# The last attention block's ending moved out of a branch and beside the following convolution; two weight sets and one table given other times and places

## The chip, the cores and the metric

The kernel runs on one core of one Trainium2 chip. The metric is the time of one execution in device microseconds (us). The engines are named as in the profile: PE (TensorE, with PEld for its weight loads), DVE (VectorE), ACT (ScalarE), POOL (GpSimd) and SP (SyncE, which here only issues DMA transfers). L-numbers are lines of the kernel before.

## What is computed

Four layers run one after another on two images of 128 channels and 64 x 64 pixels (L = 4096 positions). Only the end of layer 0, the start of layer 1 and one weight set of layer 2 matter here. Cut to that, the reference is:

```
# layer 0: group norm, rotary attention with 4 heads of 32 channels, projection, residual
xi = group_norm(x).reshape(b, c, L)
q, k, v = split(einsum('oc,bcl->bol', w_qkv, xi) + b_qkv)
q, k = rotary(q), rotary(k)                      # t * cos + swap(t) * sin
weight = softmax(einsum('bct,bcs->bts', qh * scale, kh * scale))
a = einsum('bts,bcs->bct', weight, vh).reshape(b, c, L)
x = xi + einsum('oc,bcl->bol', w_proj, a) + b_proj

# layer 1 (its start): a 3x3 convolution 128 -> 64 with GELU (the stem), then a wide 9x9 one, and others
h = gelu(affine(conv2d(x, cv1_w, 1)))
o0 = silu(affine(conv2d(h, conv0_w, 4)))
...

# layer 2: three residual steps with two 3x3 convolutions, weights w1 and w2
for _ in range(3):
    x = x + (conv(relu(conv(x, w1) + b1), w2) + b2) / 3
```

## The kernel before, in words

The image stays in memory all the time as `xa` (128 channels on the partitions, both images, with a border of one pixel).

**Prologue of layer 0** (`layer0`, 0 to 102 us). SP loads the two images in quarters (`load_x`, L121) and the table of cosines and sines in eight slices (`load_cs`, L124) into the tile `cs`, 32 KB per partition. ACT's queue loads the small weights, among them `wvT`, `wprojT` (L88) and `wproj3` (L90; only the branch that is not taken uses it). DVE takes the statistics (L143), ACT normalises, and for 16 steps PE multiplies q and k, DVE rotates them with the cosines (L186, L188), POOL adds (L190, into five buffers rt3) and SP stores them to DRAM. The values of the first image are split into three bf16 parts and a column of ones (`v3[0]`, `v3[1]`; POOL sets the ones, L136, two memsets).

**The branch.** A flag computed from the data decides between `attend` (taken) and `attend_any` (L297). Everything inside is one unit: nothing outside the branch is put between its instructions, and behind it every engine jumps over the code of the other side.

**`attend`** goes over image b, head h, block qb of 512 queries and 32 blocks kb of 128 keys, in groups of three kb, in an order written out by hand. For a group PE makes the scores (L382), ACT the exponentials (L388), and two groups later PE accumulates the weighted values (L398). Since `v3` has columns of ones, the accumulator has three partial sums of 32 rows and the denominators in the last 32. At kb = 31 `normalise` makes the quotient of the head: a reciprocal (L409), two copies, three products on DVE (L415), two additions on POOL (L416, L417) into `att`. When all four heads of a block are there, `project` multiplies with `wpt` (PE, L424) and DVE adds the residual and the bias `bo` to `xa` (L426); this is done at kb = 24 of the next block, and for the very last block (b = 1, qb = 7) behind the loop, with nothing beside it. SP fetches pieces of q and k for the next head into a ring of two (`stg`), POOL and DVE split them (L346, L353). The second image's values are made inside this loop (`late_values`, for h = 1 and 2 of the first image).

**Behind the branch** (`body`, then `layer1`). ACT's queue loads `w1T` (L1964), and DVE makes layer 2's first weights `u1` of it (`quad_weights`, ten instructions, L1093 to L1102). SP loads the stem's weights `cv1T` (L588) into memory that later is `comb[5]`, then the wide convolution's weights `conv0T` in 18 loads (L595) and stores the image for later (`xs`, L597). POOL clears the border of `hz` (L600). Then, in an order written out by hand, the stem goes over eight blocks of eight rows: 36 matmuls each (L627), a Gelu on ACT (L632); between the blocks DVE prepares the wide convolution's weights (`wide_weights`, L607 to L618) and combinations of the stem's output (`combine`, L644 to L651). The wide convolution's products follow on PE (L667). The stem's block k reads rows 8k - 1 to 8k + 8 of both images.

Of the kernel before, what the change touches and what calls it, by code (L numbers as in the profile page):

```python
# [10 lines left out]
F32 = mybir.dt.float32  # L11
F16 = mybir.dt.float16
# [8 lines left out]
P = 128  # L21
# [53 lines left out]
def layer0(g, I):  # L75
# [6 lines left out]
    with ExitStack() as ctx:  # L82
# [3 lines left out]
        nc.scalar.dma_start(wv, I["wvT"])  # L86
        wpt = w.tile([P, P], F32, name="wpt")
        nc.scalar.dma_start(wpt, I["wprojT"])  # L88
        wp3 = w.tile([96, NH, P], F32, name="wp3")
        nc.scalar.dma_start(wp3, I["wproj3"])  # L90
        flag = w.tile([1, 1], I32, name="flag")
        bo = w.tile([P, 1], F32, name="bo")

# [8 lines left out]
        with ExitStack() as pctx:  # L102
# [11 lines left out]
            top = pw.tile([P, NB, 2, NBLK], F32, name="top")  # L114
            cs = pw.tile([P, NBLK, 2, BLK], F32, name="cs")

# [14 lines left out]
            for k in range(1, NBLK):  # L131
                load_cs(k)
            bv = pw.tile([P, 1], F32, name="bv")
            nc.scalar.dma_start(bv, I["bv"].unsqueeze(1))
            for b in range(NB):
                nc.gpsimd.memset(v3[b][:, :, :, 3 * CH :], 1.0)  # L136

# [159 lines left out]
        with tc.If(small > 0) as cond:  # L297
            attend(g, v3, wv, wpt, bo, qd, kd, q4, qk, stg)
        with cond.Else():
            with tc.tile_pool(name="l0vs", bufs=2) as vs, tc.tile_pool(name="l0vp", bufs=2, space=PSUM) as vp:  # L300
                for k in range(NBLK):
                    late_values(g, v3, vp.tile([P, BLK], F32, name="pv"), vs, wv, 1, k)
            attend_any(g, v3, wp3, bo, qd, kd, q4)

# [5 lines left out]
def fetch(g, stg, src, n, c):  # L310

    b, h = divmod(n, NH)
    t = stg.tile([P, PIECE], F32, name="piece")
    for r in range(4):
        g.nc.sync.dma_start(
            t[r * CH : (r + 1) * CH], src[b][h * CH : (h + 1) * CH, c * PIECE : (c + 1) * PIECE]
        )
    return t


# [40 lines left out]

def attend(g, v3, wv, wpt, bo, qd, kd, q4, qk, stg):

# [5 lines left out]
    with ExitStack() as ctx:  # L369
# [23 lines left out]
        def weigh(group, e):  # L393
            nonlocal acc
            for i, (b, h, qb, kb) in enumerate(group):
                if kb == 0:
                    acc = psa.tile([P, BLK], F32, name="acc")
                nc.tensor.matmul(acc, v3[b][:, kb, h, :], e[:, i, :], start=(kb == 0), stop=(kb == NS - 1))  # L398
                if kb == NS - 1:
                    normalise(b, h, qb, acc)  # L400
                    if h == NH - 1:
                        done.append((b, qb))

        def normalise(b, h, qb, acc):

            if qb == h == 0:
                att[b] = ap.tile([P, L], F32, name="att")
            rec = sm.tile([96, BLK], F32, name="rec")
            nc.vector.reciprocal(rec[0:32], acc[96:128])  # L409
            nc.vector.tensor_copy(rec[32:64], rec[0:32])  # L410
            nc.vector.tensor_copy(rec[64:96], rec[0:32])
            parts = sm.tile([CH, 3, BLK], F32, name="parts")
            for j in range(3):
                rows = slice(32 * j, 32 * j + 32)
                nc.vector.tensor_tensor(parts[:, j, :], acc[rows], rec[rows], ALU.mult)  # L415
            nc.gpsimd.tensor_add(parts[:, 0, :], parts[:, 0, :], parts[:, 1, :])  # L416
            nc.gpsimd.tensor_add(  # L417
                att[b][h * CH : (h + 1) * CH, qb * BLK : (qb + 1) * BLK], parts[:, 0, :], parts[:, 2, :]
            )

        def project(b, qb):

            pp = psa.tile([P, BLK], F32, name="acc")
            nc.tensor.matmul(pp, wpt, att[b][:, qb * BLK : (qb + 1) * BLK], start=True, stop=True)  # L424
            xv = interior(g, b, qb * RB, RB)
            nc.vector.scalar_tensor_tensor(xv, img(pp), bo, xv, ALU.add, ALU.add)  # L426

# [12 lines left out]
        ]  # L440
        held, done, coming = [], [], []
        with tc.manual_schedule():
            for c in range(1, 4):
                split_less(g, qk[0], 1, c, q4[1][:, c * PIECE : (c + 1) * PIECE], nc.vector)
            for u in range(0, len(units), GR):
                group = units[u : u + GR]
                b, h, qb, kb = group[0]
                held.append((group, scores(group)))
                if done and 24 <= kb < 24 + GR:
                    project(*done.pop(0))  # L450
                if len(held) > LAG:
                    weigh(*held.pop(0))
                if b == 0 and 1 <= h <= 2 and qb in (0, 5, 6, 7) and 24 <= kb < 24 + GR:
                    k = 4 * (h - 1) + (0, 5, 6, 7).index(qb)
                    late_values(g, v3, psa.tile([P, BLK], F32, name="acc"), sm, wv, 1, k)
                if 4 <= kb < 4 + GR:
                    coming = [(n, j, c, fetch(g, stg, (qd, kd)[j], n, c)) for n, j, c in pieces(b * NH + h, qb)]
                elif 26 <= kb < 26 + GR:
                    for n, j, c, t in coming:
                        split(g, qk[n % 2], j, c, t)  # L460
                    coming = []
            for x in held:
                weigh(*x)
            for x in done:
                project(*x)


def attend_any(g, v3, wp3, bo, qd, kd, q4):

    nc, tc = g.nc, g.tc  # L470
    NS = L // P
    with ExitStack() as ctx:
        big = ctx.enter_context(tc.tile_pool(name="l0big", bufs=1))
        sm = ctx.enter_context(tc.tile_pool(name="l0sm", bufs=2))
        at = ctx.enter_context(tc.tile_pool(name="l0at", bufs=2))
        pss = ctx.enter_context(tc.tile_pool(name="l0ps2", bufs=2, space=PSUM))
        pst = ctx.enter_context(tc.tile_pool(name="l0pst", bufs=2, space=PSUM))
        pso = ctx.enter_context(tc.tile_pool(name="l0pso", bufs=1, space=PSUM))
        id16 = big.tile([P, P], F16, name="id16")
        nc.vector.tensor_copy(id16, g.ident)  # L480

        for b in range(NB):
# [34 lines left out]
            for qt in range(NS):  # L517
                aT = sm.tile([96, NH, P], F32, name="aT")
                for h in range(NH):
                    s16, nm, e16 = scores(qt, h)  # L520
                    nc.scalar.activation(e16, s16, AF.Exp, bias=nm)
                    pt = at.tile([P, NS, P], F16, name="pt")
                    for j in range(4):
# [15 lines left out]
                xv = interior(g, b, qt * 2, 2)  # L539
                nc.vector.scalar_tensor_tensor(xv, img(pp), bo, xv, ALU.add, ALU.add)  # L540

# [23 lines left out]
def stem_and_wide(g, I, hz, fw, early, ahead):  # L565
# [14 lines left out]
    with ExitStack() as ctx:  # L580
# [6 lines left out]
        cw = comb[5].rearrange("p q r i -> p (q r i)")[:, : 9 * 64].rearrange("p (t o) -> p t o", o=64)  # L587
# [1350 lines left out]
def body(ctx, tc, I, out, layers=(0, 1, 2, 3), dump=None):  # L1938
# [156 lines left out]
```

## Time and profile before

| what | value |
|---|---|
| median of 3 runs | 5540.79 us (5538.51 to 5542.69) |
| the profiled execution | 5536.55 us |
| its span in the profile | 5534.8 us |
| mean granted PE clock | 0.886 |
| busy PE, DVE, ACT, POOL | 85%, 82%, 74%, 66% of the span |
| attention, first score to last accumulation | 103.1 to 1038.1 us |
| stem (L627) | 1056.4 to 1121.3 us |
| wide convolution, first product | 1121.3 us |

The span is the time from the first to the last instruction on the core; the rest of the execution's time lies around it. "Busy" sums an engine's instructions over the span, so it is an average over stages with different limits. The chain of waits follows the work that ended last backwards; a row of it gives start, length and what it was. In a group's row, `out<-in` are the tiles, `x` the number of instructions, then follow busy time, the mean of one in ns, and the idle time before them with what ended it. Queue rows (PEldq, SPq and so on) are the instructions of an engine's sequencer, such as jumps, semaphore waits and DMA issues.

### The profile page before, as it was taken

The page shows a single profiled execution, that of the slowest core. Times are in us where ns is not written, and L with a number is a line of the kernel's source. Part 1 is how long each engine was busy: PE and PEld are TensorE (multiplying, and loading weights), DVE is VectorE, ACT ScalarE, POOL GpSimd, SP SyncE. Part 2 cuts the span into 40 slices and gives each one's busy share as a digit, 9 for nine tenths or more (in the row PEclk, how much of TensorE's full clock was granted, in tenths as well). Part 3 has the DMA queues.
Part 4 walks back from the last instruction along what each step waited for, and adds up shares of the span by engine and source line. Part 5 has one row for each costly group of instructions (what it writes and reads, how often), then busy time and mean ns, then how long its engine had stood idle before and what let it go on. Part 6 is the DMA issues. An engine that isn't in the chain of part 4 may idle for free.

```text
span 5534.8 us, 54557 instructions
## 1 busy us (share of the span) xinstructions
PE 4701.0 (85%) x17062; PEld 1747.6 (32%) x17062; DVE 4548.0 (82%) x4253; ACT 4072.5 (74%) x6257; POOL 3646.3 (66%) x1196
## 2 busy tenths in 40 slices
PE   7999999899987899778888778778888777788776
PEld 3444444344443343222222222222222222222221
DVE  7665555551346996899999999999999999999998
ACT  4999999500346213798888888888888888888886
POOL 5222222100001211899999999999999999999998
PEclk9999999999998999888787888887887889888887
DMA  4111111300563000655655555555565565555554
GB/s 169 43 46 31 31 31 39 62 1 16 110 108 75 10 0 6 147 128 127 148 130 132 138 141 127 134 143 131 139 144 132 127 146 132 133 135 142 138 131 103
DMA packets 335737, 554.27 MB, mean 100 GB/s; under 512 B 69600, under 2 KB 116208, under 8 KB 335440
## 3 DMA queue, kind: packets, MB, share of 16 engines
q1 hardware_dynamic: 334032, 549.27, 41.8%
q8 instruction: 135, 2.21, 0.2%
q10 hardware_dynamic: 1408, 1.46, 0.1%
q14 instruction: 162, 1.33, 0.1%
HBM read 461.40 MB, written 89.13 MB: 99 GB/s over the span
## 4 chain that ended last, share of the span: by engine, by line
DVE 45%; PE 35%; ACT 10%; issue 5%; DMA 2%; POOL 1%; SPq 0%; DVEq 0%; POOLq 0%; ACTq 0%
DVE db L1682 30%; DVE db L1646 11%; PE ps L382 8%; PE acc L398 8%; PE m L1236 6%; PE m L667 4%; ACT da L1668 4%; PE acd L973 2%; DVE gt L1709 1%; ACT db L1674 1%; PE m L627 1%; PE pf L936 1%; ACT L1533 1%; ACT u L1533 1%; PE m L806 1%
## 5 line engine op out<-in xcount | busy, mean ns | idle before, releaser
L1692 POOL TENSOR_TENSOR db<-db,c 128x2048 f32<-128x2048 f32 x512 | 2312.5, 4531 | 45.6 <-ACT hl L1687 32.2
L1668 ACT ACTIVATE da<-dd,am 128x512 f32<-128x512 f32 x2048 | 1398.1, 687 | 301.1 <-DVE db L1682 280.4
L1682 DVE TENSOR_TENSOR_SCAN db<-da,db 128x512 f32<-128x512 f32 x1376 | 1583.9, 1201 | 34.5 <-ACT db L1674 26.9
L388 ACT ACTIVATE e<-ps 128x1536 f16<-128x1536 f32 (+1 forms) x683 | 919.7, 1601 | 23.2 <-PE ps L382 23.2
L1682 DVE TENSOR_TENSOR_SCAN db<-da,hl,db 128x512 f32<-128x512 f32 x672 | 825.9, 1271 | 40.9 <-POOL db L1655 2.8
L1646 DVE TENSOR_TENSOR db<-pbc,dd 128x2048 f32<-128x2048 f32 (+1 forms) x384 | 779.6, 2030 | 31.8 <-DMA dd<-dx 31.8
L1655 POOL TENSOR_TENSOR db<-b,dd 128x2048 f32<-128x2048 f32 (+1 forms) x192 | 772.9, 4026 | 14.0 <-DMA b<-bx 14.0
L1700 PE MATMUL py<-db,fold 128*32 128x512 f32 x4096 | 610.7, 682 | 150.9 <-POOL db L1692 150.8
L382 PE MATMUL ps<-q 128*128 128x512 f16 x2048 | 553.0, 378 | 3.4 <-issue 2.1
L398 PE MATMUL acc<-e,v 128*128 128x512 f16 x2048 | 552.9, 379 | 0.1
L416 POOL TENSOR_TENSOR parts<-parts 32x512 f32<-32x512 f32 x64 | 80.4, 1257 | 666.3 <-DVE parts L415 650.3
L1674 ACT ACTIVATE db<-da,db,hl 128x1 f32<-128x1 f32 x1120 | 393.7, 352 | 147.4 <-DVE db L1646 103.5
L1287 POOL MEMSET v<- 128x256 f32 x2 | 1.1, 550 | 699.7 <-DVE b L1125 699.7
L1236 PE MATMUL m<-v,u 128*128 128x512 f32 x864 | 378.1, 600 | 42.9 <-DVE v L1179 41.3
L409 DVE RECIPROCAL rec<-acc 32x512 f32<-32x512 f32 x64 | 214.9, 3358 | 212.0 <-PE acc L398 211.7
L1593 PE MATMUL pm<-dd,ident 128*128 128x512 f32 x512 | 356.5, 834 | 2.9 <-ACT dd L1586 2.7
L1625 PE MATMUL pbc<-bc,sel 64*128 64x512 f32 x384 | 208.7, 543 | 127.7 <-DVE db L1646 126.9
L1552 PE MATMUL pm<-u,wxp 128*72 128x512 f32 x256 | 191.3, 890 | 141.0 <-ACT u L1533 141.0
L382 PEld LDWEIGHTS <-q 128*128 128x128 f16 x2048 | 197.3, 97 | 273.4 <-issue 92.8
L398 PEld LDWEIGHTS <-v 128*128 128x128 bf16 x2048 | 199.0, 97 | 248.4 <-issue 9.1
L1700 PEld LDWEIGHTS py<-db,fold 128*32 128x32 f32 x4096 | 90.4, 114 | 542.9 <-issue 309.3
L1528 PE MATMUL pm<-xn,wcs 128*128 128x512 f32 x512 | 235.1, 602 | 18.5 <-ACT xa L1727 7.3
(342 smaller groups left out, 6575.7 us busy)
## 6 DMA issues: line engine op xcount, KB each, us to landing
dd<-dx SPq DMA_DIRECT2D x1024, 256.0 KB, 6.5
dx<-dd SPq DMA_DIRECT2D x128, 512.0 KB, 5.5
c<-bx SPq DMA_DIRECT2D x1024, 64.0 KB, 2.1
b<-bx SPq DMA_DIRECT2D x512, 64.0 KB, 4.6
early<-pos SPq DMA_DIRECT2D x104, 256.0 KB, 9.8
piece<-qd SPq DMA_DIRECT2D x128, 128.0 KB, 2.7
piece<-kd SPq DMA_DIRECT2D x112, 128.0 KB, 2.7
hats<-pos SPq DMA_DIRECT2D x32, 256.0 KB, 9.8
```

Source lines behind the costliest of these rows:

```text
L382: nc.tensor.matmul(ps[:, i, :], t[:, 1, kb * P : (kb + 1) * P], t[:, 0, qb * BLK : (qb + 1) * BLK], start=True, stop=True,)
L388: nc.scalar.activation(e[:, :n, :], ps[:, :n, :], AF.Exp, scale=1.0 / UP**2)
L398: nc.tensor.matmul(acc, v3[b][:, kb, h, :], e[:, i, :], start=(kb == 0), stop=(kb == NS - 1))
L1236: nc.tensor.matmul(m[x], weights[j][:, dy, x, :], v[j][b][:, x, r0 : r0 + RP, :].rearrange("p r i -> p (r i)"), start=(dy == 0), stop=(dy ...
L1593: nc.tensor.matmul(ps, g.ident, S[i]["dd", hf][:, x, :], start=(x == 0), stop=(x == 1))
L1646: nc.vector.tensor_tensor(db_tile(k)[:, :, :n], G[k].pop("pb")[:, :n].unsqueeze(1).to_broadcast([P, 4, n]), S[i]["d4", hf][:, 1, :, :n], A ...
L1655: nc.gpsimd.tensor_tensor(db_tile(k)[:, :, n:], S[i]["b", ng][:, n:].unsqueeze(1).to_broadcast([P, 4, BLK - n]), S[i]["d4", hf][:, 1, :, n ...
L1668: nc.scalar.activation(da, S[i]["d4", hf][:, 0, q, :], AF.Exp, scale=am[:, hf, q, ng : ng + 1])
L1674: nc.scalar.activation(b0, da[:, first : first + 1], AF.Identity, bias=b0, scale=hl[:, hf, ng, q, :])
L1682: nc.vector.tensor_tensor_scan(d1, d0, d1, 0.0 if zero else hl[:, hf, ng, q, :], ALU.mult, ALU.add)
L1692: nc.gpsimd.tensor_mul(v, v, S[i]["c", ng].unsqueeze(1).to_broadcast([P, 4, BLK]))
L1700: nc.tensor.matmul(S[i]["y", hf][32 * q : 32 * q + 32, :], fold, G[k]["db"][:, q, :], start=False, stop=(ng == NNG - 1),)
```

## The change

- **The last block's ending.** `normalise` and `project` become functions of the module. In the branch, the last block's first three heads are normalised into `g.heads` instead of `att`; of the last head ACT only copies the accumulator, denominators included, to `g.last`. Behind the branch, ahead of the stem's first block, DVE and POOL normalise it into `g.heads` with the stem's later buffers as scratch. After the stem's second block (k = 1) PE projects, DVE adds the residual, and SP stores the second image (`xs[1]`), which before was stored together with the first.
- **The stem's weights.** `cv1T` is loaded at the start of the kernel, on SP's queue behind the cosines, into `g.cw`.
- **One tile for all of it.** `g.lead`, 1728 columns, lives from before layer 0 to the end of layer 2: columns 0 to 575 are `cw`, 576 to 1087 `last`, 1088 to 1599 `heads`, the rest `wpt`. All of it later serves as `comb[5]`. `u1` and `bo` live there too now.
- **Layer 2's weights.** `w1T` is fetched in three parts (three taps of 128 columns each) into the ring of the q and k pieces, in the blocks qb = 5, 6, 7 of the first image's last head, and each part is made into weights there.
- **The cosines.** `cs` is no tile of its own but the memory of `v3[1]`, seen as float32. The ones of `v3[1]` are set by POOL at the start of `attend`.
- **Smaller ones.** `wproj3` is loaded only in the branch that is not taken. The scratch of `late_values` shares a ring with the reciprocals. The other branch sets `last` and `heads` so that the ending adds only the bias.

The core of the diff:

```
 def layer0(g, I):
-        wpt = w.tile([P, P], F32, name="wpt")
+        wpt, bo = g.wpt, g.bo
         nc.scalar.dma_start(wpt, I["wprojT"])
-        wp3 = w.tile([96, NH, P], F32, name="wp3")
-        nc.scalar.dma_start(wp3, I["wproj3"])
-        bo = w.tile([P, 1], F32, name="bo")
...
-            cs = pw.tile([P, NBLK, 2, BLK], F32, name="cs")
+            cs = v3[1].bitcast(F32).rearrange("p s h d -> p (s h d)").rearrange("p (k i c) -> p k i c", k=NBLK, i=2)
...
                 load_cs(k)
+            nc.sync.dma_start(g.cw, I["cv1T"])
...
-            for b in range(NB):
-                nc.gpsimd.memset(v3[b][:, :, :, 3 * CH :], 1.0)
+            nc.gpsimd.memset(v3[0][:, :, :, 3 * CH :], 1.0)

+def residual_taps(g, I, pool, y):
+    t = pool.tile([P, PIECE], F32, name="piece")[:, : 3 * P].rearrange("p (x o) -> p x o", o=P)
+    g.nc.sync.dma_start(t, I["w1T"][:, 3 * y : 3 * y + 3, :])
+    return t
+def residual_weights(g, y, t):
+    quad_weights(g, g.u1[:, y : y + 1], t.unsqueeze(1), 1.0)
+def normalise(g, acc, rec, parts, dst):
+    nc = g.nc
+    nc.vector.reciprocal(rec[0:32], acc[96:128])
+    nc.vector.tensor_copy(rec[32:64], rec[0:32])
+    nc.vector.tensor_copy(rec[64:96], rec[0:32])
+    for j in range(3):
+        rows = slice(32 * j, 32 * j + 32)
+        nc.vector.tensor_tensor(parts[j], acc[rows], rec[rows], ALU.mult)
+    nc.gpsimd.tensor_add(parts[0], parts[0], parts[1])
+    nc.gpsimd.tensor_add(dst, parts[0], parts[2])
+def project(g, b, qb, pp, att):
+    g.nc.tensor.matmul(pp, g.wpt, att, start=True, stop=True)
+    xv = interior(g, b, qb * RB, RB)
+    g.nc.vector.scalar_tensor_tensor(xv, img(pp), g.bo, xv, ALU.add, ALU.add)

 def late_values(g, v3, pv, pool, wv, b, k):
-    v32 = pool.tile([P, 4, NH, CH], F32, name="v32")
+    v32 = pool.tile([P, BLK], F32, name="rec").rearrange("p (c h d) -> p c h d", c=4, h=NH)

 def attend(g, I, v3, wv, qd, kd, q4, qk, stg):
+        def finish(b, h, qb, acc):
+            final = (b, qb) == (NB - 1, NBLK - 1)
+            if final and h == NH - 1:
+                nc.scalar.copy(g.last, acc)
+                return
+            to = g.heads if final else att[b][:, qb * BLK : (qb + 1) * BLK]
+            rec = sm.tile([P, BLK], F32, name="rec")
             parts = sm.tile([CH, 3, BLK], F32, name="parts")
+            normalise(g, acc, rec, [parts[:, j, :] for j in range(3)], to[h * CH : (h + 1) * CH])
+            if h == NH - 1:
+                done.append((b, qb))
...
         with tc.manual_schedule():
+            nc.gpsimd.memset(v3[1][:, :, :, 3 * CH :], 1.0)
...
                 if 4 <= kb < 4 + GR:
                     coming = [...]
+                    if (b, h) == (0, NH - 1) and qb >= 5:
+                        taps = qb - 5, residual_taps(g, I, stg, qb - 5)
                 elif 26 <= kb < 26 + GR:
...
+                    if taps:
+                        residual_weights(g, *taps)
+                        taps = None
             for x in held:
                 weigh(*x)
-            for x in done:
-                project(*x)

 def stem_and_wide(g, I, hz, fw, early, ahead):
-        comb = [early[:, i] for i in range(5)] + [a.tile([P, NQ, CR, NF], F32, name="comb5")]
-        cw = comb[5]...
-        nc.sync.dma_start(cw, I["cv1T"])
+        comb = [early[:, i] for i in range(5)] + [g.lead.rearrange("p (q r i) -> p q r i", q=NQ, r=CR)]
+        cw = g.cw
...
-        for b in range(NB):
-            nc.sync.dma_start(g.xs[b].rearrange("c (h w) -> c h w", w=HW), interior(g, b))
+        nc.sync.dma_start(g.xs[0].rearrange("c (h w) -> c h w", w=HW), interior(g, 0))
...
         with tc.manual_schedule():
+            s, p, d, q = spdq[0]
+            normalise(g, g.last, s, [t[0:CH] for t in (p, d, q)], g.heads[3 * CH :])
             for k in range(NBLK):
                 stem(k)
+                if k == 1:
+                    project(g, NB - 1, NBLK - 1, ps.tile([P, BLK], F32, name="m"), g.heads)
+                    nc.sync.dma_start(g.xs[1].rearrange("c (h w) -> c h w", w=HW), interior(g, 1))

 def body(ctx, tc, I, out, layers=(0, 1, 2, 3), dump=None):
-    if 0 in layers:
+    with tc.tile_pool(name="l2w", bufs=1) as pool:
+        g.u1 = pool.tile([P, 3, 6, P], F32, name="u1")
+        g.bo = pool.tile([P, 1], F32, name="bo")
+        g.lead = pool.tile([P, 1728], F32, name="lead")
+        g.cw = g.lead[:, : 9 * 64].rearrange("p (t o) -> p t o", o=64)
+        g.last = g.lead[:, 576:1088]
+        g.heads = g.lead[:, 1088:1600]
+        g.wpt = g.lead[:, 1600:]
         layer0(g, I)
-    with tc.tile_pool(name="l2w", bufs=1) as pool:
-        with tc.tile_pool(name="l2stage", bufs=1) as stage:
-            raw = stage.tile([P, 9, P], F32, name="raw")
-            nc.scalar.dma_start(raw, I["w1T"])
-            g.u1 = pool.tile([P, 3, 6, P], F32, name="u1")
-            quad_weights(g, g.u1, raw.rearrange("p (y x) o -> p y x o", x=3), 1.0)
```

More of the change, by code (lines that the diff above doesn't have):

```diff
@@ L297, in layer0 @@
         with tc.If(small > 0) as cond:
-            attend(g, v3, wv, wpt, bo, qd, kd, q4, qk, stg)
+            attend(g, I, v3, wv, qd, kd, q4, qk, stg)
         with cond.Else():
+            nc.gpsimd.memset(v3[1][:, :, :, 3 * CH :], 1.0)
             with tc.tile_pool(name="l0vs", bufs=2) as vs, tc.tile_pool(name="l0vp", bufs=2, space=PSUM) as vp:
@@ L302, in layer0 @@
                     late_values(g, v3, vp.tile([P, BLK], F32, name="pv"), vs, wv, 1, k)
-            attend_any(g, v3, wp3, bo, qd, kd, q4)
+                for y in range(3):
+                    residual_weights(g, y, residual_taps(g, I, vs, y))
+            nc.vector.memset(g.last[0:96], 0.0)
+            nc.vector.memset(g.last[96:128], 1.0)
+            nc.vector.memset(g.heads, 0.0)
+            attend_any(g, I, v3, qd, kd, q4)
 PIECE = L // 4
@@ L359, in split, with attend @@
     split_less(g, qk, j, c, t, g.nc.vector)
-def attend(g, v3, wv, wpt, bo, qd, kd, q4, qk, stg):
+def attend(g, I, v3, wv, qd, kd, q4, qk, stg):
     nc, tc = g.nc, g.tc
@@ L399, in weigh @@
                 if kb == NS - 1:
[L400 to L404, printed above, removed]
+                    finish(b, h, qb, acc)
+        def finish(b, h, qb, acc):
             if qb == h == 0:
                 att[b] = ap.tile([P, L], F32, name="att")
[L408 to L411, printed above, removed]
-            parts = sm.tile([CH, 3, BLK], F32, name="parts")
[L413 to L426, printed above, removed]
+            final = (b, qb) == (NB - 1, NBLK - 1)
[4 more added lines that the diff above has]
+            rec = sm.tile([P, BLK], F32, name="rec")
+            parts = sm.tile([CH, 3, BLK], F32, name="parts")
+            normalise(g, acc, rec, [parts[:, j, :] for j in range(3)], to[h * CH : (h + 1) * CH])
+            if h == NH - 1:
+                done.append((b, qb))
         def pieces(n, qb):
@@ L441, in attend @@
         held, done, coming = [], [], []
+        taps = None
         with tc.manual_schedule():
+            nc.gpsimd.memset(v3[1][:, :, :, 3 * CH :], 1.0)
             for c in range(1, 4):
@@ L449, in attend @@
                 if done and 24 <= kb < 24 + GR:
-                    project(*done.pop(0))
+                    b0, q0 = done.pop(0)
+                    project(g, b0, q0, psa.tile([P, BLK], F32, name="acc"), att[b0][:, q0 * BLK : (q0 + 1) * BLK])
                 if len(held) > LAG:
@@ L461, in attend, with attend_any @@
                     coming = []
+                    if taps:
+                        residual_weights(g, *taps)
+                        taps = None
             for x in held:
                 weigh(*x)
-            for x in done:
-                project(*x)
-def attend_any(g, v3, wp3, bo, qd, kd, q4):
+            assert not done
+def attend_any(g, I, v3, qd, kd, q4):
     nc, tc = g.nc, g.tc
@@ L475, in attend_any @@
         at = ctx.enter_context(tc.tile_pool(name="l0at", bufs=2))
+        tp = ctx.enter_context(tc.tile_pool(name="l0tp", bufs=1))
         pss = ctx.enter_context(tc.tile_pool(name="l0ps2", bufs=2, space=PSUM))
@@ L478, in attend_any @@
         pso = ctx.enter_context(tc.tile_pool(name="l0pso", bufs=1, space=PSUM))
+        wp3 = big.tile([96, NH, P], F32, name="wp3")
+        nc.scalar.dma_start(wp3, I["wproj3"])
         id16 = big.tile([P, P], F16, name="id16")
@@ L521, in attend_any @@
                     nc.scalar.activation(e16, s16, AF.Exp, bias=nm)
-                    pt = at.tile([P, NS, P], F16, name="pt")
+                    pt = tp.tile([P, NS, P], F16, name="pt")
                     for j in range(4):
@@ L539, in attend_any @@
                 xv = interior(g, b, qt * 2, 2)
-                nc.vector.scalar_tensor_tensor(xv, img(pp), bo, xv, ALU.add, ALU.add)
+                if b == NB - 1 and qt >= NS - BLK // P:
+                    nc.vector.tensor_add(xv, xv, img(pp))
+                else:
+                    nc.vector.scalar_tensor_tensor(xv, img(pp), g.bo, xv, ALU.add, ALU.add)
 def layer1(g, I):
@@ L584, in stem_and_wide @@
         spdq = [[a.tile([P, BLK], F32, name=f"{n}{b}") for n in "spdq"] for b in range(NB)]
-        comb = [early[:, i] for i in range(5)] + [a.tile([P, NQ, CR, NF], F32, name="comb5")]
-        cw = comb[5].rearrange("p q r i -> p (q r i)")[:, : 9 * 64].rearrange("p (t o) -> p t o", o=64)
-        nc.sync.dma_start(cw, I["cv1T"])
+        comb = [early[:, i] for i in range(5)] + [g.lead.rearrange("p (q r i) -> p q r i", q=NQ, r=CR)]
+        cw = g.cw
         w = a.tile([P, K9, NQ, NX, P], F32, name="w9")
```

## The prediction

> **What bounds it now.** I read four views: the page's chain, the chain of waits around the end of layer 0, the view of the branch's line (L297), and the stretches table. Through attention and stem the chain is TensorE's (PE) nearly without a break; the one long break lies between them. The chain of waits from the last accumulation to the stem (start, us, what; lines left out):
>
> ```profile
> 1037.50 0.61 PE acc L398 x2
> ...
> 1038.13 3.37 DVE rec L409
> ...
> 1045.22 1.26 POOL att L417
> ...
> 1046.53 2.09 PE acc L424 x2
> ...
> 1049.47 5.73 DMA raw<-in_w1T
> ...
> 1056.44 8.59 PE m L627 x25
> ```
>
> The last block's quotient (DVE, then POOL), its projection (PE), the residual (DVE) and a load stand one behind another: PE goes from 1038.11 to 1056.44, 18.3 us, with only the 2.1 us projection in it. The load drawn is w1T, but the stem does not need it. What it needs is cv1T, issued by SP at 1049.53 into memory that the attention held; its last packet lands at 1055.78, and PE starts 0.66 later.
>
> What a jump out of the branch costs each engine, so what becomes late next:
>
> ```profile
> L297 PEldq COMPARE_BRANCH  x2: 92/1732/3373, 102.5 to 1046.5; - x2
> L627 PEldq EVENT_SEMAPHORE  x7: 51/51/51, 1050.0 to 1056.3; - x7
> ```
>
> (duration in ns min/median/max, first and last start). PE's jump began at 1046.53, when the last wait of its code in the branch (for the quotient) was met, and took 3.37 us, to 1049.90; now it hides behind the load. Then come seven semaphore instructions, about 0.1 us each when already met.
>
> **The branch's end, step by step.** The change puts quotient, projection and residual of the last block behind the join, beside the stem, and loads cv1T at the start. PE's last wait inside the branch is then for the last weights, met at 1037.50. Jump to 1040.87, seven semaphores 0.7: the stem starts at **1041.6** instead of 1056.44, **14.8 us** earlier. Nothing else is later: ACT's new copy of the accumulator starts at 1038.11 and takes 0.59 to 0.64 (L716, the same shape), the residual of the block before ended at 1034.5, and cv1T has landed long ago. Without the jump's cost the start would be the copy's end plus semaphores, about 1039.5: 2.1 us more gain, an end of the range.
>
> The stem's length: from its second block on, the Gelus (L632) start 7.73 apart; eight blocks are 61.8. Over the whole chain its entry is 64.84 (288 matmuls), so the half clock at its start cost 3.0. Here are clock rows (us, then columns as PE, PEld, DVE, ACT, POOL, then PEclk, DMA):
>
> ```profile
> 1056.40:1062.10 5.70, 5.66 (x14) 1.94 (x16) 4.34 (x9) 0.00 (x0) 0.98 (x4) 0.50 1.22 206
> 1062.10:1067.20 5.10, 5.10 (x26) 1.85 (x24) 2.71 (x2) 0.00 (x0) 0.14 (x1) 1.00 1.20 210
> 1590.30:1593.70 3.40, 0.03 (x2) 0.00 (x0) 1.40 (x2) 3.22 (x4) 0.00 (x0) 1.00 0.50 51
> 1593.70:1598.00 4.30, 3.82 (x5) 1.48 (x6) 3.08 (x4) 1.37 (x2) 0.00 (x0) 0.61 0.82 89
> 1643.20:1646.50 3.30, 0.00 (x0) 0.00 (x0) 1.40 (x2) 3.19 (x3) 0.00 (x0) 0.90 0.50 56
> 1646.50:1652.70 6.20, 6.18 (x50) 3.97 (x50) 3.35 (x4) 0.97 (x2) 0.00 (x0) 0.50 0.83 124
> ```
>
> PE's new gap is 1038.1 to 1041.6, 3.5 us. Gaps of 3.4 and 3.3 us are followed in these rows by half clock for about 3.4 us (0.61 over 4.3) and 6.2 us: a cost of 1.7 or 3.1; none is the other bound. I take 1.7, the nearest in length. The projection on PE adds 0.9 (warm pairs of L424 are 0.86). Stem end: 1041.6 + 61.8 + 1.7 + 0.9 = **1106.0**; now it is 1056.44 + 64.84 = 1121.3. **Gain 15.3**, between 13.9 and 19.1 by these bounds.
>
> The Trainium skill (TensorE: Matmul & The Clock Gate, Part 1) has the clock fall only after one whole idle window of about 3.4 us, on a grid that runs on freely. By that rule most positions of a 3.5 us gap contain no whole window, the clock stays up, and the gain is 17.0 instead of 15.3. The rows speak against it: both gaps are shorter than the window and the clock fell.
>
> What hides the moved work: stem(0) and stem(1) need no row of the last block; only stem(6) does, some 46 us in. The quotient takes 8.4 us now (1038.13 to 1046.49), so is done about 1047.3; PE projects after stem(1), about 1059; DVE adds the residual when its work on stem(0) is done, about 1060; stem(6) starts near 1091. POOL's memsets of hz (1.1 us) no longer wait for w1T.
>
> DVE must have the first wide weights and combinations ready at the stem's end. Now it starts them at 1064.45, when six conv0T loads are there, ends them at 1101.6, and 19.7 us remain. SP issues those loads from about 1039 instead of 1049.95, without w1T and cv1T ahead of them (0.86 MB at 210 GB/s, 4 us): start near 1050, plus 37.2, plus 0.8 residual, ends at 1088, 18 us before the stem's end. Hidden; were that cover gone, PE would wait for the rest.
>
> **Inside the attention.** Three times a 196 KB load and ten DVE instructions of 128 (or 256) columns. At 0.39 (L645, the dearest row of that width) a set is 3.9 us. The three blocks they go into are busy 7.2, 6.8 and 7.0 us of 14.4 to 14.6 on DVE, and SP has no piece to fetch there: cost 0; if an accumulator had to wait, at most 3.9 per block. Merging v32 with rec shares a ring of two whose users lie a block apart: 0.
>
> At the attention's start POOL gets a memset of 3.51 us (L136), beside DVE's first three L353, of which PE already waits 0.8 us for one. In DVE's rows of L353, beside POOL's casts the mean is 1858 against 1223 alone:
>
> ```profile
> L353 DVE TENSOR_TENSOR q<-piece,q 64x1024 f16<-64x1024 f32 x19 | 35.3, 1858 | 46.1 <-POOL q L346 45.9
> L353 DVE TENSOR_TENSOR q<-piece,q 64x1024 f16<-64x1024 f32 x1 | 1.2, 1223 | 0.0
> ```
>
> If the memset held DVE up whole, the first L353 ends near 107.3 instead of 104.0 and PE's third group, at 106.16, would wait 1.3. If not, nothing. I take **0.3 lost**. The Trainium skill (SBUF — State Buffer, DVE and GpSimd sharing a port) says that a two-input DVE instruction meets only GpSimd instructions that read SBUF; a memset only writes. By that the loss is 0; no row here shows a memset beside such an instruction.
>
> **The prologue.** wproj3 (192 KB) leaves ACT's queue, cv1T (288 KB) joins SP's behind the cosines.
>
> SP's and DVE's timeline (start, us):
>
> ```profile
> 0.73 7.03 SPq L121 DMA_DIRECT2D q<-in_x  x4
> ```
> ```profile
> 12.60 1.29 DVE L143 BATCH_NORM_STATS2 st<-q 128x6 f32<-128x512 f32 x2 [1.16 <-DMA q<-in_x]
> ```
>
> The four loads of the first image are issued at 0.73, 1.18, 5.43 and 7.43; the last two wait until an earlier load's semaphore is free (vecs at 5.42, wprojT at 7.42). One load fewer ahead frees one such place: the third could go at once and the fourth between 5.2 and 7.4. The statistics' last wait ends at 12.60, and PE is the chain from 18.2 on. Gain 0 to 2.2; against it cv1T, 1.4 us of transfer (w's loads of that size come 1.4 apart), which could delay the first q and k stores. Five rt3 buffers hide that; if they don't, 1.4 is lost. I take **0.6 gained**.
>
> The cosines in v3[1]: 0 if their slices are waited for one by one, as now (the first L186 runs at 21.64, the last cosine load is issued only at 19.1 and lands 7 us or more later). 6.75 KB per partition now lies below hz instead of beside w9, which moves later tiles over others' memory: 0, plus or minus 1.5, about the waits at layer borders.
>
> **Sum.** 15.3 + 0.6 - 0.3 = 15.6. The profiled execution took 5536.55 (span 5534.8 and 1.75 around it) and would take 5521.0; the runs' median, 5540.79, lies 4.2 above it, so **5525.2** (-0.28%).
>
> **Rivals.**
> *The stem waits for the quotient after all*: g.lead is one tile (cv1T, accumulator, heads), and if it is tracked whole, the first stem matmul waits for POOL's last add, 1038.1 + 0.6 + 8.4 = 1047.1. With 0.1 more, a cold start of 3.0, 61.8 and 0.9 the stem ends at 1112.9: gain 8.4, with prologue and memset 8.7, **5532**. Against: PE multiplies with slices of w (L667, idle 0.0) while DVE writes other slices (L613 to L618). Chance 0.08.
>
> *The cosines are tracked whole in the bitcast tile* (that part doesn't do what it says): the first rotation waits for the last load, 19.1 + 7 to 10.6 (median to landing), so 27 to 29.7 instead of 21.6, 8 lost at most: gain 7.6, **5533**. Against: q4 is used under two types, and attention starts while its other pieces are still being written. Chance 0.07.
>
> *The jump starves* (the other side): the 18 conv0T loads now start at the moment in which PE, ACT and DVE fetch code behind the join. Now PE jumps with the DMA engines idle (share 0.01 before 1041.7). If the code came behind these loads, which now take 31.7 us from first issue to last landing, the stem would start at 1070.6, 14.2 later than now; with 0.9 and 0.3, **5556**. It turns slower from a delay of some 15 us. Against: between 1040 and 1130 the instruction queue's packets took 1.15 us each beside these loads (0.4% of 16 engines' 90 us, 5 packets), and the jump begins before SP's first issue. Chance 0.05.
>
> *New waits further on*, from the moved memory or the renumbered queues, 5 to 20 us: **5530 to 5545**. For: the profile can't exclude it; against: ring sizes stay. Chance 0.07.
>
> The forecast has 0.73; its own range is 5521 to 5529 (bounds of clock, jump and prologue). The range that holds 8 in 10 reaches to the first two rivals: 5519 to 5534. A measurement here can tell about 0.2% (11 us) from no change. Faster by more: 0.74. Within: 0.18 (two rivals, 0.03 of the last). Slower: 0.08 (the starved jump, 0.03 of the last; its remaining 0.01 stays faster).
>
> **What would show it.** The stem's first matmul 3 to 4 us after the last accumulation, PE's jump 3.4 us, PEclk 0.5 for about 3.4 us, then eight stems of 7.73; L667 starting at the stem's end without idle; the residual of the last block near 20 us into the stem; the first rotation still near 21 us. Wrong if PE's first stem wait ends on POOL or DVE, or if L667 waits for DVE or SP.

## The result, and the profile after

| | before | after |
|---|---|---|
| median | 5540.54 us (9 runs, 5537.94 to 5542.69) | 5525.0 us (9 runs, 5522.41 to 5528.26) |
| ratio, 95% interval | | 0.9973 [0.9963, 0.9983] |
| the profiled execution (its span) | 5536.55 (5534.8) | 5523.33 (5521.5) |
| mean granted PE clock | 0.886 | 0.893 |
| flag that decides the branch, end | 101.89 | 103.26 |
| last accumulation, end | 1038.09 | 1039.70 |
| stem's first product | 1056.44 | 1042.65 |
| wide convolution's first product | 1121.21 | 1105.82 |
| last accumulation to wide convolution | 83.12 | 66.12 |

The changed kernel is faster by 15.5 us or 0.28%, and the forecast was 5525.2. The sum came out; several of its terms did not. The wide convolution's start is given here by its first product; the chain's piece of the stem ends at 1121.28, hence the 1121.3 of the table before. From the last accumulation on, the new lines answer to those of before (accumulation L398 is now L433, stem L627 is L661, projection L424 is L351, the branch L297 is L294). The chain of waits of the changed kernel (start, us, what):

```profile
1039.11 0.60 PE acc L433 x2
1039.71 0.02 issue
1039.74 0.59 ACT lead L443
1040.33 2.32 issue
1042.65 15.67 PE m L661 x72
1058.32 1.06 PE m L351 x2
1059.38 10.87 PE m L661 x49
```

The quotient, the additions and the residual have left the chain; the projection stands in it with 1.06 us, between stem blocks, and nothing else of the old ending does. What is left of the gap is "issue", a time for which the profile shows no releaser. The branch's and the stem's queue rows (ns min/median/max, first and last start) say what it is:

```profile
L294 PEldq COMPARE_BRANCH  x2: 92/1732/3373, 103.9 to 1039.1; - x2
L661 PEldq EVENT_SEMAPHORE  x1: 51/51/51, 1042.5 to 1042.5; - x1
```

PE's jump starts at 1039.1, when its last wait in the branch is met, takes 3.37 us as before, and ends at 1042.5; one semaphore instruction follows, not seven.

The waits around the end (engine line <- releaser: us in total, times, longest) show where the moved work waits now:

```profile
DVE w L641 <- DMA w<-in_conv0T: 7.7, 1, 7.7
...
POOL p L345 <- issue: 5.2, 1, 5.2
DVE s L339 <- ACT lead L443: 4.3, 1, 4.3
PE m L661 <- issue: 2.9, 1, 2.9
```

DVE and POOL still wait, but beside a PE that multiplies. The stretches view (PE, PEld, DVE, ACT, POOL, then PEclk, DMA share, GB/s) for the gap, the first 7.85 us after it and the whole stem:

```profile
1039.70:1042.65 2.95, 0.00 (x1) 0.03 (x1) 2.24 (x1) 0.58 (x1) 1.12 (x4) 1.00 0.21 56
1042.65:1050.50 7.85, 7.85 (x38) 3.21 (x40) 3.98 (x6) 0.00 (x0) 2.96 (x2) 1.00 1.21 195
1042.65:1105.80 63.15, 63.15 (x290) 21.79 (x290) 53.63 (x97) 6.72 (x8) 2.96 (x2) 1.00 0.72 119
```

In the third row PE is busy for the whole stem, 288 stem products and the projection's two, at full clock; before, the stem's first 5.7 us ran at half clock.

From the wide convolution's start on, the two traces run 15.4 us apart through that whole stage. Beyond it the difference wanders between about 12.6 and 18 and ends at 13.2. I don't read the wandering as the change: three profiles of the changed kernel itself take 1070.5, 1074.3 and 1075.7 us from the wide convolution to layer 3. But the two profiles of the kernel before take 1069.4 and 1071.7 there, so that a loss of some 3 us behind the wide convolution is not excluded.

### The profile page after: what moved, and what is told of

Read it like the earlier page. It is cut to its first block, busy times and chain, and to the rows that moved or that the text cites. A ratio compares the mean times of both kernels' runs of the same rounds, so it can differ in the third digit from the quotient of the medians.

```text
span 5521.5 us, 54590 instructions
## 1 busy us (share of the span) xinstructions
PE 4679.6 (85%) x17062; PEld 1745.0 (32%) x17062; DVE 4550.6 (82%) x4273; ACT 4072.8 (74%) x6258; POOL 3647.7 (66%) x1196
## 4 chain that ended last, share of the span: by engine, by line
DVE 44%; PE 36%; ACT 10%; issue 5%; DMA 2%; POOL 2%; SPq 0%; DVEq 0%; POOLq 0%; ACTq 0%
DVE db L1721 30%; DVE db L1685 10%; PE ps L417 8%; PE acc L433 8%; PE m L1275 6%; PE m L701 5%; ACT da L1707 4%; PE acd L1012 2%; ACT db L1713 1%; DVE gt L1748 1%; PE m L661 1%; ACT L1572 1%; ACT u L1572 1%; PE pf L975 1%; POOL db L1731 1%
## 5 line engine op out<-in xcount | busy, mean ns | idle before, releaser
L1739 PE MATMUL py<-db,fold 128*32 128x512 f32 x4096 | 597.3, 668 | 152.1 <-POOL db L1731 152.1
L433 PE MATMUL acc<-e,v 128*128 128x512 f16 x2048 | 553.2, 379 | 0.1
L1591 PE MATMUL pm<-u,wxp 128*72 128x512 f32 x256 | 179.8, 842 | 140.7 <-ACT u L1572 140.7
L433 PEld LDWEIGHTS <-v 128*128 128x128 bf16 x2048 | 199.1, 97 | 248.9 <-issue 9.9
L1567 PE MATMUL pm<-xt,wcs 128*128 128x512 f32 x512 | 236.2, 604 | 21.3 <-ACT xa L1764 12.5
```

The costliest lines, as they stand in the source:

```text
L1739: nc.tensor.matmul(S[i]["y", hf][32 * q : 32 * q + 32, :], fold, G[k]["db"][:, q, :], start=False, stop=(ng == NNG - 1),)
```

## Experiments

Each kernel was compared with the kernel before on the same chip, and each ratio is against the runs of before taken with it (medians 5541.56 us for e2 to e4, 5540.65 for e5 to e7, 5542.94 for e9); the first row has those of the result. First an overview by stage, from one profile each ("gap" is last accumulation to the stem's first product; "stem" from there to the wide convolution; us throughout):

| kernel | median; ratio [95%] | first q product to flag | gap | stem | gap and stem |
|---|---|---|---|---|---|
| before | 5540.5 | 83.69 | 18.35 | 64.77 | 83.12 |
| before, second profile (e10) | 5539.4, one run | 84.35 | 18.10 | 63.42 | 81.52 |
| after | 5525.0; 0.9973 [0.9963, 0.9983] | 84.92 | 2.95 | 63.17 | 66.12 |
| after, second profile (e8) | 5532.3, one run | 85.93 | 3.21 | 64.87 | 68.07 |
| after, third profile (e11) | 5527.3, one run | 85.17 | 2.89 | 63.17 | 66.06 |
| e9: before, cv1T in its own memory | 5536.4; 0.9988 [0.9979, 0.9997] | 84.64 | 12.24 | 64.85 | 77.10 |
| e4: after, ending ahead of the stem | 5534.3; 0.9988 [0.9979, 0.9997] | 85.17 | 11.60 | 63.67 | 75.27 |
| e3: after, w1T behind the branch | 5532.0; 0.9982 [0.9973, 0.9991] | 85.18 | 3.45 | 70.06 | 73.50 |
| e2: after, cv1T behind the branch | 5525.8; 0.9971 [0.9960, 0.9983] | 84.93 | 3.07 | 63.16 | 66.23 |
| e5: after, branch the other way round | 5526.2; 0.9974 [0.9964, 0.9984] | 84.52 | 0.67 | 63.17 | 63.84 |
| e6: after, no branch | 5525.8; 0.9972 [0.9961, 0.9982] | - | 0.67 | 63.17 | 63.84 |
| e7: after, PE warmed at the start | 5528.1; 0.9976 [0.9967, 0.9985] | 82.89 | 3.26 | 64.74 | 68.00 |

### Which part brings what

**cv1T alone (e9).** The kernel before; the stem's weights get their own tile, and the cosines move into `v3[1]` as in the change, to make room. (The tile without that move, e1, gave no time: it does not fit. A later pool needs 36 KB per partition, and 34.3 KB were left.)

```
-        layer0(g, I)
     with tc.tile_pool(name="l2w", bufs=1) as pool:
+        g.cw = pool.tile([P, 9, 64], F32, name="cw")
+        layer0(g, I)
...
-        cw = comb[5].rearrange(...)
+        cw = g.cw
         nc.sync.dma_start(cw, I["cv1T"])
```

> The kernel before, in which the stem's weights cv1T get memory of their own (a tile made ahead of layer 0) and the cosines lie in v3[1] to make room for it; the load stays behind the branch in the code, and ending and w1T stay as before. Theory: what held cv1T until 1049.5 in the kernel before was its memory, not its place behind the branch; with memory of its own it is issued long before the join, PE's start then hangs on quotient, jump and semaphores (8.4 + 3.4 + 0.7 = 12.5 after the last accumulation instead of 18.3), the stem starts about 1050.6, and the time is about 5.8 shorter (5534.7). Rival: the load was only the last of several waits; DVE's ten instructions on w1T, or the residual of the last block, hold the stem's first product at about 1055, and the gain is under 1.5. Prologue: as in the kernel before if the grid of the clock's windows allows it, up to 1.5 later otherwise.

The gap is 12.24. Gap and stem are 6.0 shorter than in the first profile of before and 4.4 shorter than in the second; the median is 6.5 below that of the runs of before beside it. Its chain of waits, and PE's row of the branch:

```profile
1039.84 3.37 DVE rec L409
...
1046.94 1.26 POOL att L417
1048.20 0.04 issue
1048.24 2.09 PE acc L424 x2
1050.33 0.02 issue
1050.36 0.76 DVE xa L426
1051.12 0.93 issue
1052.05 12.96 PE m L628 x45
```
```profile
L296 PEldq COMPARE_BRANCH  x2: 92/1922/3753, 104.2 to 1048.2; - x2
```

With the load gone, the quotient of the old ending is the chain, and behind it comes PE's jump. The view draws the projection and the residual there, but they end at 1051.12; the jump starts with the quotient, 8.43 us after the last accumulation, takes 3.75 and ends at 1051.99, and the first stem product follows at 1052.05. So the path is the forecast one, with a longer jump (3.75 instead of 3.4) and no semaphores (0.06 instead of 0.7). The rival, DVE's ten instructions on w1T, does not show. And SP's queue shows why the load is early:

```profile
35.71 0.32 SPq L190 DMA_DIRECT2D qd<-rt  x1
36.08 2.07 SPq L589 DMA_DIRECT2D cw<-in_cv1T  x1
```

The load stands behind the branch in the code, and in SP's queue it stands at 36 us, 1000 us before the join: with memory of its own it had nothing to wait for and was put ahead of the whole branch. What had held it was its memory.

**cv1T's place (e2).** The changed kernel with the load back at its old line.

```
-            nc.sync.dma_start(g.cw, I["cv1T"])
...
         cw = g.cw
+        nc.sync.dma_start(cw, I["cv1T"])
```

> The changed kernel with one part undone: cv1T is loaded behind the branch again, first on SP's queue. Theory: SP is released by the copy of the accumulator, about 1.0 us after the last accumulation; the load needs 6.3 us until its last packet (as before) and PE 0.1 to 0.7 more, so the stem starts 7.4 to 8.0 us after the last accumulation instead of 2.9, and after such a gap at half clock for some 5 us (cost 2 to 3): 6.5 to 8 us slower than the change, about 5532. Rival (the ending outside the branch is worth the whole gain, the load hides behind PE's jump): as the change, 5525.

My theory of a late load fell: gap 3.07, time as the changed kernel's. In the trace SP issues the load at 35.1, so this kernel too has it early; the new line in the prologue buys nothing that the new tile does not. It costs nothing either: first q product to flag is 84.93 without it and 84.92 with it.

**w1T inside the attention (e3).** The changed kernel, with w1T loaded and made into weights behind the branch as before.

```
-                    if (b, h) == (0, NH - 1) and qb >= 5:
-                        taps = qb - 5, residual_taps(g, I, stg, qb - 5)
...
         layer0(g, I)
+        with tc.tile_pool(name="l2stage", bufs=1) as stage:
+            raw = stage.tile([P, 9, P], F32, name="raw")
+            nc.scalar.dma_start(raw, I["w1T"])
+            quad_weights(g, g.u1, raw.rearrange("p (y x) o -> p y x o", x=3), 1.0)
```

> The changed kernel with one part undone: w1T is loaded on ACT's queue and made into weights by DVE behind the branch, as before. Theory: ACT can issue the load only after its jump (about 3.3 us after the last accumulation), it lands 5.7 later, and DVE's ten instructions (5.1 us) stand ahead of the last block's quotient in DVE's order; the quotient is ready some 23.5 us after the last accumulation instead of 9.9, PE reaches the projection behind the second block at 18.6 and waits 5 us, then runs cold for 3.4 us (1.7): 5 to 7 us slower than the change, about 5531. Rival (DVE is not the bound beside the stem, so its place costs nothing): as the change, 5525.

The mechanism is confirmed, and the size lies a little above the forecast 5 to 7: gap and stem are 7.4 longer (73.50 against 66.12). The load took 9.75 us instead of 5.7. DVE's first weight instruction, queued ahead of the quotient's copies, waits for the load, and the quotient behind it; its waits:

```profile
DVE u L1128 <- DMA raw<-in_w1T: 8.8, 1, 8.8
...
PE m L349 <- POOL lead L344: 3.5, 1, 3.5
```

PE reaches the projection 3.5 us too early and stands. To that come 0.5 in the gap (the jump took 3.87 us here) and twice 1.7 for the clock, which was at half from 1045.3 to 1048.7 and from 1065.8 to 1069.2.

**The ending beside the stem (e4).** The changed kernel, with projection and residual ahead of the stem's first block instead of behind its second.

```
+            project(g, NB - 1, NBLK - 1, ps.tile([P, BLK], F32, name="m"), g.heads)
             for k in range(NBLK):
                 stem(k)
-                if k == 1:
-                    project(g, NB - 1, NBLK - 1, ps.tile([P, BLK], F32, name="m"), g.heads)
```

> The changed kernel with the projection and the residual of the last block ahead of the stem's first block instead of behind the second. Theory: the ending is worth something only beside PE work; PE waits for the quotient (9.9 us after the last accumulation), projects cold (2.1), and the stem starts 12.1 after the last accumulation instead of 2.9 and runs cold for about 5 us: 9 to 11 us slower than the change, about 5535. Rival (leaving the branch is what counts): as the change, 5525.

Confirmed: 9.2 longer (75.27), with the wait where it was to be:

```profile
PE m L351 <- POOL lead L346: 9.6, 1, 9.6
```

Leaving the branch before the quotient brings little by itself; the 9 us come from PE having something to do meanwhile. So the parts need each other: cv1T alone stands at 77.1 (e9), everything but the work beside the stem at 75.3 (e4), everything but w1T inside the attention at 73.5 (e3), all together at 66.1. What cv1T's own memory is worth beside the moved ending is not shown: e2 was to undo it, and undid only the load's line.

### Is the rest of the gap the jump?

**Branch the other way round (e5)** and **no branch (e6).** In e5 the test is inverted, so that the code of `attend` comes second and its end falls through. In e6 the flag is still made but not read, and the other side is left out.

```
-        with tc.If(small > 0) as cond:
-            attend(g, I, v3, wv, qd, kd, q4, qk, stg)
-        with cond.Else():
+        with tc.If(small < 1) as cond:
...
+        with cond.Else():
+            attend(g, I, v3, wv, qd, kd, q4, qk, stg)
```

> The changed kernel with the branch's sides exchanged (condition negated): the attention is the far side, reached by a jump, and falls through at its end. Theory (the 2.9 us gap at the join is the jump over the other side's code): the gap shrinks to about 0.7 to 1.0 (semaphores, or the copy's end), 2 us less, and the first score comes 2.5 to 3.5 us later after the flag than now (1.3 us), in all 0 to 2 us slower than the change, 5525 to 5527. Rival (the gap is the join's semaphore waits): gap still 2.9, entry as now, 5525.

> The changed kernel without the branch: the attention is run whatever the flag says, the flag is made and not read, and the other side is left out. Theory: no jump, so 2 us less at the join (gap 0.7 to 1.0 at most, set by the semaphores and the copy), and 1 to 3 us less at the entry, because no engine waits for the flag: 3 to 5 us faster than the change, about 5521. Rival (what is left at the join is the ending itself, not the branch): no gain there, 5524 to 5525.

Both gaps are 0.67, most of it ACT's copy of the accumulator (0.59), so 2.3 of the 2.95 us are the jump. With the jump at the join the gap follows its length: jumps of 3.31, 3.37, 3.49, 3.63, 3.69 and 3.87 us (e11, after, e2, e8, e7, e3) go with gaps of 2.89, 2.95, 3.07, 3.21, 3.26 and 3.45. But neither kernel gains. In e5 the jump is taken at the attention's entry instead:

```profile
L294 PEldq COMPARE_BRANCH  x1: 3941/3941/3941, 104.0 to 104.0; - x1
```

From the flag to the first scores it takes 4.83 us instead of 1.09, and 2.3 saved stand against 3.7 lost. In e6 the forecast 3 to 5 us did not come, since the entry costs as much in another way: without the border of the branch, the attention's first instructions are mixed into the prologue's end (POOL's 3.51 us memset of `v3[1]` at 99.88 stands ahead of the last addition of the rotation, at 103.35), and from the first q product to the last accumulation it takes 1023.9 instead of 1021.4 us. The granted clock is also at half for longer there, from 95.5 to 112.5 instead of 98.8 to 109.1; what each of the two costs was not separated.

### The prologue's 1.4 us

The flag came 1.37 us later after the change. The first eight q and k products hold it: the chains of the kernel before, of its second profile, and of the changed kernel:

```profile
18.20 5.12 PE pq L184 x8
23.32 1.02 PE pm L325 x16
```
```profile
18.94 5.66 PE pq L184 x8
24.61 1.02 PE pm L325 x16
```
```profile
18.34 6.36 PE pq L181 x8
24.70 1.03 PE pm L360 x16
```

The same eight products take 5.12, 5.66 and 6.36 us. In the clock records full speed comes 2.9, 4.0 and 5.4 us after the first product: the longer the half clock, the longer the products, at half a us per us.

**Second and third looks (e10, e11, e8)**: the kernel before once more, and the changed kernel twice more, each unchanged.

> The kernel before, once more, for its prologue. Theory: the 1.4 us that the flag came later after the change is the clock's grid, not the change: from the first q product to the flag's end it takes 83.7 plus half of whatever the clock needs beyond 2.9 us to reach full speed, and in another profile of the same kernel that is anything up to 85.2. Rival: it is the change (the renumbered loads), and the kernel before shows 83.7 with full clock after 2.9 again.

> The changed kernel once more, for its prologue and its gap. Theory (grid): first q product to flag between 83.5 and 86, by half of the clock's start-up; gap 2.9 to 3.5 us, clock kept or fallen, stem to wide 63.2 or 64.8. Rival (change): 84.9 again.

> The changed kernel once more, for a second profile. Theory (the prologue and the stem's start depend on where the clock's grid stands, which no run repeats): everything up to 18.3 us and every distance that holds no clock change is the same within 0.1 us; the flag lies anywhere from 101.8 to 103.4, and the stem takes 63.2 (clock kept) or 64 to 65 (clock fallen in the 2.9 us gap). Rival (the prologue lost 1.4 us to the renumbered loads): the flag at 103.1 again.

The flag ends at 103.29 in the second profile of before and at 103.26, 103.64 and 103.19 in the three of the changed kernel. By 83.69 plus half of what the clock needs beyond 2.88 us, first product to flag would be 84.2 in e10 (measured 84.35), 84.6 in e9 (84.64), 84.9 in the changed kernel (84.92) and 85.1 in e11 (85.17); e8, whose clock fell again within the prologue, lies 0.7 above. One expectation fell: up to the first product the profiles do not agree within 0.1 us. In e8 it starts at 17.27 instead of 18.34, because the image's last part is there at 11.67 instead of 12.75.

The grid can be read from the records: in every trace all changes of the granted clock, 360 or more, lie whole multiples of 3.413 us apart. In all profiles but that of e7 the clock first rises at the end of the first such step with at least 2.88 us of q products in it: 2.88 were enough in the kernel before, and 2.63 were not in e8, where it rose one step later. So the place of the first product on the grid holds the first difference, as the theory said. The start-up was longer in all three profiles of the changed kernel (5.4, 6.0 and 5.7 us) than in the two of before; but e6, with the same code up to there, needed 3.3, so it isn't always so. Whether the change makes a long start-up more likely stays open.

**A warm start (e7).** The changed kernel, with 18 and then 8 products added on PE among the statistics, whose results nobody uses.

```
                 norm_mean(0)
+                warm(18)
                 norm_spread(0)
                 norm_root(0)
+                warm(8)
```

> The changed kernel with 26 small matmuls more on PE (identity by identity into an unused PSUM tile) ahead of the first q and k products, 18 before and 8 behind the group sums. Theory (the prologue's 1.4 us were lost by where the clock's grid stood: half speed for 5.4 us after 18.3 instead of 2.9): the first products run at full clock whatever the grid, and the flag comes at about 100.5, 2.6 earlier than in the change's profile and 1.3 earlier than in that of before; in all 1 to 2.6 us faster than the change, 5523. Rival (the prologue lost its 1.4 us to the renumbered loads or to cv1T): the flag stays at 103.1, 5525.

It failed. Nothing held the first set back, so it ran from 5.55 to 12.51, too soon: the clock was full from 11.2 to 14.6 and then at half until 21.4. The second set stood in the way:

```profile
16.65 3.62 PE pq L218 x16
20.27 4.08 PE pq L181 x8
```

The eight products now take 4.08 instead of 6.36 us, but start 1.9 later; the flag is 0.3 earlier, and the kernel is not faster.

## Why the prediction was right, and where it was not

- **The gap.** Predicted 3.5, measured 2.95, 2.89 and 3.21. The mechanism was right: nothing but PE's own jump was late next (3.37 us, in e5 and e6 0.67 without it). The mis-sized term was the semaphores: I carried over seven (0.7), and there is one (0.17 from the jump's end to the first product).
- **The clock after the gap.** Predicted a cost of 1.7, bounds 0 and 3.1. Measured 0 in two profiles of the changed kernel and 1.7 in the third, which shows exactly the predicted picture:

```profile
1042.68:1043.90 1.22, 1.22 (x6) 0.54 (x8) 1.19 (x2) 0.00 (x0) 0.00 (x0) 1.00 1.18 221
1043.90:1047.30 3.40, 3.40 (x10) 1.20 (x8) 2.54 (x5) 0.00 (x0) 1.31 (x1) 0.50 1.22 195
1047.30:1050.70 3.40, 3.40 (x18) 1.37 (x16) 0.00 (x0) 0.00 (x0) 1.65 (x2) 1.00 1.22 199
```

  (e8, columns as above.) Ten products instead of eighteen in the middle 3.4 us. It was wrong to price the gap by one number from the nearest row: in one and the same kernel it cost 0 twice and 1.7 once. What decides is not shown. Of the six gaps near 3 us in these profiles the three longest lost the clock and the three shortest kept it, so their length would explain it as well as their place on the grid. By the rule of the Trainium skill that the prediction weighed (TensorE: Matmul & The Clock Gate, Part 1), a fall needs one whole idle window of about 3.4 us. The two profiles that kept the clock agree with it; e8 and e7 do not, since their gaps of 3.21 and 3.26 us are shorter than such a window and the clock fell all the same.
- **Projection on PE, and the stem.** Predicted 0.9, measured 1.06. Without it and with the clock kept the stem takes 62.1, where the sum had 61.8.
- **Hidden work.** Right: PE has no idle time at the wide convolution's start, DVE's residual runs at 1064.0 (predicted about 1060) and its first wide weights at 1054.53 (predicted near 1050); the part that the prediction let end at 1088 ends at 1089.9, 16 us before the stem does. e3 shows the price when DVE is not free: 7.4.
- **Inside the attention.** Predicted 0, measured 935.35 against 935.03 from first score to last accumulation. The 0.3 are not w1T's: e3, without w1T there, takes 935.48.
- **The memset at the entry.** Predicted 0.3 lost, measured nothing: flag to first score 1.09 against 1.17. DVE's and POOL's timelines (start, us):

```profile
104.19 3.50 DVE L388 TENSOR_TENSOR q<-q,q 64x1024 f16<-64x1024 f32 x3 [0.93 <-DVE flag L291]
```
```profile
103.99 3.51 POOL L468 MEMSET v<- 128x4096 bf16 x1 [3.26 <-DVE flag L291]
```

  Three instructions in 3.50 us beside the memset, 1221 ns each in their row: as fast as the same three before, without the memset (1221). The Trainium skill (SBUF — State Buffer, Who interferes with whom) was right here, and my row, taken beside casts, was not comparable.
- **The prologue.** Predicted 0.6 gained; as a whole this step failed, even in sign. The freed place on the queue lets the fourth load of the first image out at 7.12, 6.42 and 7.07 in the three profiles of the changed kernel instead of 7.43 and 7.64; the third does not go at once (5.61, 4.06 and 5.54). In the first pair of profiles that brought nothing. SP's first loads and the statistics' last wait after the change:

```profile
0.73 6.71 SPq L118 DMA_DIRECT2D q<-in_x  x4
```
```profile
12.75 1.29 DVE L140 BATCH_NORM_STATS2 st<-q 128x6 f32<-128x512 f32 x2 [1.06 <-DMA q<-in_x]
```

  The four issues end 0.3 earlier, the data come 0.15 later (12.75 against 12.60). That pair misleads, though: over all profiles the data come at 12.75, 11.67 and 12.87 in the changed kernel and at 12.60 and 13.34 before, 0.5 earlier on average and so about as predicted, within a scatter of more than 1 us. What was missing in the sum is PE's cold start, which I had not priced at all: from the first q product to the flag it takes 85.3 on average after and 84.0 before, and 1.24 of the first pair's 1.37 us lie in the first eight products.
- **The sum.** By the first two profiles gap and stem gained 17.0 instead of 15.3, flag and attention lost 1.6 instead of gaining 0.3: 15.4 at the wide convolution, 15.6 predicted. These errors cancel, and the clock is in both of them. Over all profiles gap and stem take 82.3 on average before (two) and 66.8 after (three), so 15.6 less; that agreement rests on a scatter of 2 us in either kernel.
- **The rivals.** None came. The stem does not wait for POOL's last add though g.lead is one tile; the first rotation runs at 22.17, not at 27, so the cosines are waited for slice by slice; the jump took 3.37 us beside loads moving 56 GB/s in the gap and 195 GB/s right behind it, and as long before (3.37 and 3.47), so it did not starve; and new waits of 5 us and more, from the moved memory, do not show on average (1070.5 to 1075.7 us from the wide convolution to layer 3, against 1069.4 and 1071.7); smaller ones are not excluded.

## What to carry to other kernels

When a load that is needed late stands on the chain, look first at who holds the memory it goes into: here a tile of its own moved the load 1000 us ahead, and its place in the code did not matter. A serial ending (quotient, projection, residual) is worth moving only if the engine that waits has other work there and if no engine of the ending has a load's wait queued ahead of it; with one of the two missing, 9 and 7 us stayed on the chain here. Price a PE gap near 3 us with two values for the clock and a cold start with a range, and look at second profiles of both kernels before a shift of 1 us at the kernel's start is put down to the change.

## What the hardware showed that was not expected

- PE's taken jump over the other side's code took 3.29 to 3.94 us, and between 2.3 (end) and 3.7 (entry) of it could be seen in the time. The other engines' branch rows show only 0.04 to 0.07 us, but for ACT that is not all of it: its row begins at 1039.7 in the changed kernel, its copy ends at 1040.33, and its first load behind the join is issued at 1042.72, 3.0 us after the last accumulation. In e5, with no jump at that place, it is 0.5 us.
- The clock fell after PE gaps of 3.21, 3.26 and 3.45 us and stayed up after 2.89, 2.95 and 3.07. In e8 it fell at 1043.9; of the 3.4 us before that PE was idle for 2.2. In e3 (3.45) it was idle for 2.1 of them.
- From the first q product of the prologue to full clock it took between 2.9 and 6.0 us over these kernels (e7 apart), and 2.9 and 4.0 in two executions of the same one. The Trainium skill (TensorE: Matmul & The Clock Gate, Part 1) says that the windows run freely and that the number of cold products changes from run to run; these traces agree, and at half a us per us the spread here is worth up to 1.6 us per cold start.
